# A four-layer graph network on one core: layer 2's running maxima take their scalar from the logits' buffer, 25 pairs ahead

## The chip, the core and the metric

The kernel runs on one core of a Trainium2 chip. Its engines are TensorE (PE in the profile; PEld is its weight load), VectorE (DVE), ScalarE (ACT), GpSimd (POOL) and SyncE (SP, which here only issues DMAs). Each engine works through its own instructions strictly in the order in which they were laid down, and waits on semaphores of the others. The metric is the device time of one execution in microseconds (us); lower is better.

## What is computed

Four layers update x (4096 rows of 256 features) with one adjacency matrix (4096 x 4096): a gated attention layer, a mean over neighbours, a graph attention layer (layer 2) and a dot-product attention layer. The change touches only layer 2:

```
h  = relu(layernorm(x)) @ W
e  = leaky_relu(e_src[:, None] + e_dst[None, :], 0.01)
att = softmax(where(adj > 0, e, -1e12), axis=1)
x  = x + elu(att @ h)
```

Each logit is thus made of one number of its row (src) and one of its column (dst), and the softmax needs, for each row, the maximum over that row's neighbours. Since the leaky slope is monotone, this is decided by the largest dst among the neighbours.

## The kernel before

The kernel is written in a tile framework: the program is traced in Python, and then a scheduler lays each engine's instructions out. Program order is its priority, but an instruction whose inputs or whose buffer are not ready by the scheduler's own reckoning lets later ones go first, so the order in which an engine works can differ from the order in the source. Where an instruction waits on the chip, everything behind it on its engine waits too.

Layer 2 uses the class `Attention` (line 193). The 4096 rows are cut into 8 blocks of 4 row tiles (`RB`), and the columns into 32 tiles of 128 (`NT`), taken two at a time: a *pair* is one block and two column tiles, 16 pairs to a block (`PPB`), 128 pairs in all. A pair goes through these steps:

- `logits` (L348): DVE makes y, two instructions of 128x512 (L355), out of the row of the block (`ab`), the column's scalar (`cdst`) and a row `b` kept in PSUM, which is copied there once a block (L353); GpSimd subtracts the adjacency mask (L359).
- `run` (L361): three pairs later ACT takes the exponential (L387, twice), and PE multiplies by v into four accumulators (L408; 16 matmul records a pair). At a block's edges two pairs are multiplied together. After its last pair come the reciprocals (L417) and `finish2` (L961; L967 on DVE and L971 on ACT empty the accumulators, L975 to L978 do the elu and add to x). There are 5 accumulator buffers for 4 rows of a block.
- y has 8 buffers (`n_y`). A buffer comes free when PE has multiplied it.

The maxima run ahead in `reach` (L273): for each column tile one DVE instruction of 128x512, `run = min(code - dst, run)` (L290 for a block's first column, L292 after), where `dst` is a per-partition scalar, read from the tile that `dst_of` (L225) names. The last one of a block writes `run_sb` in SBUF. Then `top` (L305) is stepped once per pair by `link`: PE transposes `run_sb` (L312), DVE reduces it to one number a row and makes `ab` from it (L316 to L321), PE transposes `ab` (L324), ACT copies it (L327), and two DMAs on ACT's queue write it to memory (L341) and read it back as a row for all partitions (L343). Only then can `logits` of that block begin.

The masks and the codes for the maxima are one tile, `turned`: `stored(b, q)` (L952) loads one of 1 MB, four pairs of one block, by SP's queue into one of 8 buffers. `reach` reads it first, the mask (L359) last, and then the buffer takes the next load.

In `run`, pair n's iteration calls `reach(n + PPB + lead)`, then `logits` of pair n. `lead` is `LEAD` = 7, so the source asks for 16 + 7 = 23 pairs ahead. Ahead of `run`, beside the projections of layer 2, a loop does `reach` for pairs 16 to 22; block 0's were done in layer 1. Nothing but the codes and the run itself holds a `reach` back.

Of the kernel before, what the change touches and what calls it, by code (L numbers as in the profile page):

```python
# [16 lines left out]
ALU = mybir.AluOpType  # L17
AX = mybir.AxisListType
# [23 lines left out]
def kernel(ctx: ExitStack, tc: tile.TileContext, w: dict, out: bass.AP):  # L42
    nc = tc.nc
# [14 lines left out]
    PPB = NT // 2  # L58
# [103 lines left out]
    class Tally:  # L162

        def __init__(self, pool, bufs, lo, hi):
            self.pool, self.bufs = pool, bufs
            self.asked, self.came = [(t, q) for t in range(lo, hi) for q in range(NQ)], []
# [26 lines left out]
    class Attention:  # L193
        def __init__(self, es, tag, slope, lag, n_y, blocks, turned, finish, ps_top=None):
            self.tag, self.slope, self.lag, self.n_y = tag, slope, lag, n_y
            self.turned, self.finish = turned, finish

            self.links = []
            self.blocks = [{"at": at, "n": n} for at, n in blocks]
            vp = es.enter_context(tc.tile_pool(name=f"{tag}_sd", bufs=1))  # L200
            self.sdst = vp.tile([P, NT], F32, name="sdst")
            self.cdst = vp.tile([P, NT], F32, name="cdst")
            self.own_dst, self.held = None, False
            self.ab_d = [
                dram.tile([2, n, P], F32, name=f"{tag}_ab_d{k}") for k, (_, n) in enumerate(blocks)
            ]
            self.picks, self.spread = None, 0
            self.small = es.enter_context(tc.tile_pool(name=f"{tag}_small", bufs=4))
            self.row_p = es.enter_context(tc.tile_pool(name=f"{tag}_rows", bufs=2))
            self.ps_run = es.enter_context(tc.tile_pool(name=f"{tag}_run", bufs=1, space=PSUM))  # L210
            self.ps_top = ps_top or es.enter_context(
                tc.tile_pool(name=f"{tag}_top", bufs=1, space=PSUM)
            )
# [56 lines left out]
            nc.vector.tensor_scalar(self.sdst[:, at], dst, self.slope, None, ALU.mult)  # L270
            nc.vector.tensor_scalar(self.cdst[:, at], dst, 1.0 - self.slope, None, ALU.mult)

        def reach(self, n):  # L273

            b, c = n // PPB, n % PPB * 2
            st = self.blocks[b]
            at, n = st["at"], st["n"]
            if c == 0:  # L280
                st["run"] = self.ps_run.tile([P, RB, P], F32, tag="run", name="run")[:, 0:n, :]
            for j in range(c, c + 2):
                code = self.turned(b, j // QT)[:, :, j % QT, :]
                dst = self.dst_of(slice(j, j + 1))
                to = st["run"]
                if j == NT - 1:
                    to = self.row_p.tile([P, RB, P], F32, tag="run", name="run_sb", bufs=1)
                    to = to[:, 0:n, :]
                if j == 0:
                    nc.vector.tensor_scalar(to, code, dst, None, ALU.subtract)  # L290
                else:
                    nc.vector.scalar_tensor_tensor(  # L292
                        to, code, dst, st["run"], ALU.subtract, ALU.min
                    )
                st["run"] = to
            if c == NT - 2 and not self.held:
                self.links.append(self.top(b))
                if b == 0:
                    self.top_now()
# [61 lines left out]
        def run(self, es, lead, n_acc, ahead=lambda n: None):  # L361

            self.y_p = es.enter_context(tc.tile_pool(name=f"{self.tag}_y", bufs=self.n_y))
            self.ps_b = es.enter_context(
                tc.tile_pool(name=f"{self.tag}_b", bufs=1, space=PSUM)
            )
            ps_acc = es.enter_context(
                tc.tile_pool(name=f"{self.tag}_acc", bufs=n_acc, space=PSUM)
            )
            pairs = [(b, c) for b in range(len(self.blocks)) for c in range(0, NT, 2)]  # L370
            LAG = self.lag
            accs, held = {}, []
            ys = {}
            for n in range(len(pairs) + LAG):
                if n < len(pairs):
                    b, c = pairs[n]
                    ahead(n)
                    if n + PPB + lead < len(pairs):
                        self.reach(n + PPB + lead)
                    y = self.y_p.tile([P, RB, 2, P], F32, tag="y", name="y")  # L380
                    ys[n] = y = y[:, 0 : self.blocks[b]["n"], :, :]
                    self.logits(y, b, c, self.turned(b, c // QT))
                if n >= LAG:
                    b, c = pairs[n - LAG]
                    y = ys.pop(n - LAG)
                    for k in range(2):
                        nc.scalar.activation(  # L387
                            y[:, :, k, :], y[:, :, k, :], AF.Exp,
                            bias=self.sdst[:, c + k : c + k + 1],
                        )  # L390
                    if c == 0:
                        accs[b] = [
                            ps_acc.tile([P, D + 1], F32, tag="acc", name="acc")
                            for _ in range(self.blocks[b]["n"])
                        ]


                    held.append((c, y))
                    edge = NT - 2 - c < 4 or b > 0 and c < 4
                    if edge and len(held) < 2:  # L400
                        self.link()
                        continue
                    terms = [(r, c1 + k, y1) for r in range(len(accs[b]))
                             for c1, y1 in held for k in range(2)]
                    if not edge:
                        terms.sort(key=lambda term: term[1])
                    for r, j, y1 in terms:
                        nc.tensor.matmul(  # L408
                            out=accs[b][r], lhsT=y1[:, r, j % 2, :], rhs=self.v[:, j, 0 : D + 1],
                            start=(j == 0), stop=(j == NT - 1),  # L410
                        )
                    held.clear()
                    if c == NT - 2:
                        done = accs.pop(b)
                        rden = self.small.tile([P, RB], F32, tag="rden", name="rden")
                        for r, acc in enumerate(done):
                            nc.vector.reciprocal(rden[:, r : r + 1], acc[:, 0:1])  # L417
                        self.finish(self.blocks[b]["at"], done, rden)
                self.link()
# [43 lines left out]
    LEAD = 7  # L463
    FIRST = 8
    FRESH = 10
    with ExitStack() as l0:
# [10 lines left out]
        with ExitStack() as es:  # L477
# [24 lines left out]
            n = 2 * RB  # L502
# [458 lines left out]
    def finish2(at, accs, rden):  # L961
# [15 lines left out]
        nc.vector.scalar_tensor_tensor(e, e, 1.0, rows, ALU.min, ALU.add)  # L977
        nc.vector.scalar_tensor_tensor(rows, h, -1.0, e, ALU.max, ALU.add)  # L978

    cuts2 = [(t, RB) for t in range(0, NT, RB)]  # L980
    att2 = Attention(l2, "l2", 0.01, 3, 8, cuts2, None, finish2)
    one2 = l2.enter_context(tc.tile_pool(name="l2_one", bufs=1))
# [9 lines left out]
    def turn2(b, pst):  # L992
        h = one2.tile([P, BT, D], F32, tag="h", name="h")
        for i in range(BT):
            normed2(h[:, i, :], b * BT + i)
        return transposed_block(two2, pst, h, "hT")
# [4 lines left out]
    with ExitStack() as es:  # L1001
# [120 lines left out]
        lead = [gather(t, NB) for t in range(2)]  # L1122
# [14 lines left out]
    with ExitStack() as es:  # L1137
        att2.hold(es)
        turned_p = es.enter_context(tc.tile_pool(name="l2_turned", bufs=8))
        work2 = es.enter_context(tc.tile_pool(name="l2_work", bufs=1))  # L1140
        att2.turned, att2.held = stored, False
        with ExitStack() as ps_:
            pst = ps_.enter_context(tc.tile_pool(name="l2_pst", bufs=3, space=PSUM))
            psm = ps_.enter_context(tc.tile_pool(name="l2_psm", bufs=3, space=PSUM))

            def block2(b):
                hT = hT2.pop(b) if b in hT2 else turn2(b, pst)
                yield
                att2.project(b, hT, psm)
                yield  # L1150

            blocks = [block2(b) for b in range(NB)]
            for _ in blocks.pop(0):
                pass
            att2.links.append(att2.top(0))
            att2.top_now()
            run_staggered(blocks, 1)
            for n in range(PPB, PPB + LEAD):
                att2.reach(n)

        att2.run(es, LEAD, 5)

    l2.close()

# [232 lines left out]
```

## Time and profile before

| | us |
|---|---|
| median of 3 runs (2967.89 to 2974.53) | 2973.59 |
| the profiled execution | 2971.09 |
| its span in the trace (mean granted clock of PE 0.989) | 2969.1 |
| first and last matmul of layer 2's `run` (L408) | 1506.2 to 1995.7 |
| first and last `reach` instruction of layer 2 | 1260.9 to 1880.1 |
| PE, DVE, ACT and POOL busy, whole span | 2862.3, 1904.9, 1260.4, 960.9 |

In the lines below, a row of the timeline gives start, duration, engine, source line, operation, what it writes and reads, its shape, how many were merged, and in brackets how long the engine was idle before it and what released it. A row of the waits gives the total, the count and the longest. DVE's durations overlap by some hundredths at their ends, so the distance between starts is what an instruction costs the engine. PE's busy time is modelled and hides small gaps; the number of matmuls over a stretch of time is a better measure.

### The profile page before, as it was taken

The page shows a single profiled execution, that of the slowest core. Times are in us where ns is not written, and L with a number is a line of the kernel's source. Part 1 is how long each engine was busy: PE and PEld are TensorE (multiplying, and loading weights), DVE is VectorE, ACT ScalarE, POOL GpSimd, SP SyncE. Part 2 cuts the span into 40 slices and gives each one's busy share as a digit, 9 for nine tenths or more (in the row PEclk, how much of TensorE's full clock was granted, in tenths as well). Part 3 has the DMA queues.
Part 4 walks back from the last instruction along what each step waited for, and adds up shares of the span by engine and source line. Part 5 has one row for each costly group of instructions (what it writes and reads, how often), then busy time and mean ns, then how long its engine had stood idle before and what let it go on. Part 6 is the DMA issues. An engine that isn't in the chain of part 4 may idle for free.

```text
span 2969.1 us, 35221 instructions
## 1 busy us (share of the span) xinstructions
PE 2862.3 (96%) x13381; PEld 2336.3 (79%) x13381; DVE 1904.9 (64%) x3491; ACT 1260.4 (42%) x1922; POOL 960.9 (32%) x725
## 2 busy tenths in 40 slices
PE   7999999999999999899999998999999999999999
PEld 6888888856556666788788777888888888888888
DVE  6877767345555554577688888656765666566553
ACT  6765555389963333994354333343111112111111
POOL 6576665545543333321055555540000000000000
PEclk9999999999999999999999999999999999999999
DMA  6966654154520001796432212002111111111100
GB/s 168 224 140 136 137 127 127 44 86 78 78 47 8 8 8 22 192 243 193 144 120 79 78 65 78 29 20 82 36 62 36 38 39 58 39 34 62 34 8 8
DMA packets 109177, 238.62 MB, mean 80 GB/s; under 512 B 10752, under 2 KB 31216, under 8 KB 100304
## 3 DMA queue, kind: packets, MB, share of 16 engines
q1 hardware_dynamic: 68512, 159.34, 15.4%
q0 software_dynamic: 37696, 69.11, 15.0%
q10 hardware_dynamic: 2800, 7.92, 0.8%
q8 instruction: 105, 1.72, 0.2%
q14 instruction: 64, 0.52, 0.1%
HBM read 265.63 MB, written 37.81 MB: 102 GB/s over the span
## 4 chain that ended last, share of the span: by engine, by line
PE 67%; DVE 8%; ACT 7%; POOL 6%; issue 6%; DMA 5%; POOLq 0%; SPq 0%; DVEq 0%; ACTq 0%
PE acc L408 16%; PE acc L1329 15%; PE s L155 15%; PE mm L155 10%; PE acc L1060 8%; POOL y L359 4%; ACT sign L181 3%; DVE run L292 3%; DVE y L355 2%; DMA turned<-codesT 2%; DMA ab_row<-l_ab_d 1%; PE q_ps L155 1%; PE tp L737 1%; DMA a<-in_adj_dram 1%; DMA l_ab_d<-abT_sb 1%
## 5 line engine op out<-in xcount | busy, mean ns | idle before, releaser
L408 PE MATMUL acc<-v,y 128*128 128x257 f32 x4096 | 929.7, 386 | 13.0 <-ACT hp L971 6.3
L408 PEld LDWEIGHTS acc<-v,y 128*128 128x128 f32 x4096 | 777.9, 192 | 126.9 <-ACT hp L971 8.0
L359 POOL TENSOR_TENSOR y<-y,turned 128x1024 f32<-128x1024 f32 (+1 forms) x272 | 549.0, 2039 | 324.8 <-DVE y L355 228.8
L387 ACT ACTIVATE y<-y,sdst 128x512 f32<-128x512 f32 (+1 forms) x544 | 350.3, 689 | 421.2 <-POOL y L359 421.1
L1329 PE MATMUL acc<-v,y 128*128 128x257 f32 x2048 | 454.5, 380 | 0.4 <-DVE rden L1337 0.4
L155 PE MATMUL s<-qT,hT 128*128 128x256 f32 x2048 | 445.2, 379 | 0.7 <-ACT qT L1277 0.7
L1322 ACT ACTIVATE y<-y 128x1024 f32<-128x1024 f32 x128 | 132.2, 1055 | 714.3 <-DVE y L1321 710.0
L155 PEld LDWEIGHTS s<-qT,hT 128*128 128x128 f32 x2048 | 389.0, 190 | 54.2 <-ACT qT L1277 1.4
L1329 PEld LDWEIGHTS acc<-v,y 128*128 128x128 f32 x2048 | 387.1, 190 | 55.9 <-issue 0.8
L355 DVE SCALAR_TENSOR_TENSOR y<-ab_row,cdst,b 128x512 f32<-128x512 f32 (+1 forms) x544 | 366.3, 709 | 64.1 <-PE acc L408 55.9
L181 ACT ACTIVATE sign<-a,limits 128x1024 bf16<-128x1024 bf16 x256 | 293.9, 1148 | 20.7 <-DMA a<-in_adj_dram 15.2
L1291 DVE SCALAR_TENSOR_TENSOR y<-code,s 128x512 f32<-128x512 bf16 x256 | 175.8, 688 | 101.0 <-PE s L155 100.7
L292 DVE SCALAR_TENSOR_TENSOR run<-turned,v,run 128x512 f32<-128x512 bf16 (+1 forms) x270 | 186.5, 691 | 59.9 <-ACT turned L536 56.4
L292 DVE SCALAR_TENSOR_TENSOR run<-turned,dst,run 128x512 f32<-128x512 bf16 x240 | 180.4, 752 | 33.7 <-DMA turned<-codesT 30.1
L1321 DVE TENSOR_TENSOR y<-y,top 128x1024 f32<-128x1024 f32 x128 | 146.2, 1213 | 43.0 <-PE top L1315 43.0
L1298 DVE TENSOR_TENSOR mx<-mx,y 128x512 f32<-128x512 f32 x224 | 154.8, 691 | 7.4
L536 ACT ACTIVATE turned<-cT,log_wide 128x1024 bf16<-128x1024 bf16 x128 | 139.1, 1104 | 41.0 <-PE cT L531 32.1
L174 POOL DMA_DIRECT2D a<-in_adj_dram x128 | 76.5, 599 | 216.1 <-ACT sign L181 161.4
L155 PE MATMUL mm<-kept 128*128 128x512 f32 x288 | 136.8, 615 | 3.3 <-ACT sz L848 2.2
L1060 PE MATMUL acc<-early,eq 128*128 128x512 f32 x512 | 129.0, 401 | 6.9 <-DVE early L457 5.3
L1060 PE MATMUL acc<-late,eq 128*128 128x512 f32 x512 | 122.8, 391 | 0.0
L1060 PEld LDWEIGHTS acc<-early,eq 128*128 128x128 f32 x512 | 96.3, 190 | 30.3 <-DVE early L457 5.5
(236 smaller groups left out, 3013.1 us busy)
## 6 DMA issues: line engine op xcount, KB each, us to landing
turned<-codesT SPq DMA_DIRECT2D x36, 1024.0 KB, 4.8
adj_t<-in_adj_dram POOLq DMA_DIRECT2D x128, 256.0 KB, 5.5
codesT<-turned SPq DMA_DIRECT2D x32, 1024.0 KB, 5.5
a<-in_adj_dram POOLq DMA_DIRECT2D x128, 256.0 KB, 4.8
code<-codesT SPq DMA_DIRECT2D x128, 256.0 KB, 5.8
code<-codesT SPq DMA_DIRECT2D x64, 512.0 KB, 7.2
ab_row<-l_ab_d ACTq DMA_DIRECT2D x14, 512.0 KB, 4.7
xt<-in_x_dram SPq DMA_DIRECT2D x8, 512.0 KB, 3.8
```

Of the source, the lines that this page charges most:

```text
L155: nc.tensor.matmul(out=ps, lhsT=lhsT_of(k), rhs=rhs_of(k), start=(k == 0), stop=(k == n - 1))
L181: nc.scalar.activation(sign, self.came[g], AF.Sign, bias=limits[:, v : v + 1], accum_out=over[:, t, v, q : q + 1],)
L292: nc.vector.scalar_tensor_tensor(to, code, dst, st["run"], ALU.subtract, ALU.min)
L355: nc.vector.scalar_tensor_tensor(y[:, :, k, :], st["ab"][:, 0, :, :], self.cdst[:, c + k : c + k + 1], st["b"], ALU.add, ALU.max,)
L359: nc.gpsimd.tensor_tensor(y, y, mask[:, :, c % QT : c % QT + 2, :], ALU.subtract)
L387: nc.scalar.activation(y[:, :, k, :], y[:, :, k, :], AF.Exp, bias=self.sdst[:, c + k : c + k + 1],)
L408: nc.tensor.matmul(out=accs[b][r], lhsT=y1[:, r, j % 2, :], rhs=self.v[:, j, 0 : D + 1], start=(j == 0), stop=(j == NT - 1),)
L1060: nc.tensor.matmul(out=acc, lhsT=eqs[c // (NT // 2)][:, ts(c % (NT // 2), P)], rhs=v1[c // BT][:, c % BT, :, :], start=(c == 0), stop=(c = ...
L1291: nc.vector.scalar_tensor_tensor(y[:, :, c : c + 2, :], st["code"][:, :, c : c + 2, :], -BIG / UNIT, ps, ALU.mult, ALU.add,)
L1298: nc.vector.tensor_tensor(mx, mx, y[:, :, c : c + 2, :], ALU.max)
L1321: nc.vector.tensor_tensor(part, part, top, ALU.subtract)
L1329: nc.tensor.matmul(out=accs[r], lhsT=st["y"][:, r, c, :], rhs=v3[:, c, :], start=(c == 0), stop=(c == NT - 1),)
```

## The change

In layer 2 alone, `reach` of pair n + 25 no longer reads `dst` from its own tile. When pair n's y buffer is taken, DVE first writes the two scalars that this `reach` needs into the buffer's first two elements, by a `tensor_reduce` with a maximum over one element; the two `reach` instructions read them there, and then `logits` overwrites them. The lead of layer 2 is 9 instead of 7, in the loop ahead of `run` too (pairs 16 to 24).

```diff
-        def reach(self, n):
+        def reach(self, n, tie=None):
...
-                dst = self.dst_of(slice(j, j + 1))
+                dst = self.dst_of(slice(j, j + 1)) if tie is None else tie[:, j - c : j - c + 1]
...
                     ahead(n)
-                    if n + PPB + lead < len(pairs):
-                        self.reach(n + PPB + lead)
                     y = self.y_p.tile([P, RB, 2, P], F32, tag="y", name="y")
+                    m = n + PPB + lead
+                    if m < len(pairs) and self.tied:
+
+                        tie = y[:, 0, 0, 0:2]
+                        at = m % PPB * 2
+                        col = self.dst_of(slice(at, at + 2))
+                        nc.vector.tensor_reduce(
+                            tie, col.rearrange("p (c o) -> p c o", o=1), AX.X, ALU.max
+                        )
+                        self.reach(m, tie)
+                    elif m < len(pairs):
+                        self.reach(m)
                     ys[n] = y = y[:, 0 : self.blocks[b]["n"], :, :]
...
+    LEAD2 = 9
...
-        att2.turned, att2.held = stored, False
+        att2.turned, att2.held, att2.tied = stored, False, True
...
-            for n in range(PPB, PPB + LEAD):
+            for n in range(PPB, PPB + LEAD2):
                 att2.reach(n)
 
-        att2.run(es, LEAD, 5)
+        att2.run(es, LEAD2, 5)
```

More of the change, by code (lines that the diff above doesn't have):

```diff
@@ L203, in __init__ @@
             self.own_dst, self.held = None, False
+            self.tied = False
             self.ab_d = [
```

## The prediction, made before the result was known

> **What bounds the kernel now.** I read the page first: PE carries the span.
>
> ```profile
> PE 2862.3 (96%) x13381; PEld 2336.3 (79%) x13381; DVE 1904.9 (64%) x3491; ACT 1260.4 (42%) x1922; POOL 960.9 (32%) x725
> ```
>
> The change is in layer 2 only, so its stage decides. There the densest stretch of PE has 224 matmul records (L408) in 48.72 us, 0.217 us each; 16 records a pair make 3.47 us a pair, 55.5 us a block of 16 pairs, and 56.1 with the five transposes of `top`. All eight blocks would be 2048 x 0.217 + 7 x 0.55 = 448 us; the stage took 1995.7 - 1506.2 = 489.5. So about 41.5 us can be won at most. To see where they lie I cut the stage at PE's transpose of `ab` (L324), once a block, and asked for busy times (columns: window, its length, then busy PE, PEld, DVE, ACT, POOL).
>
> ```profile
> 1539.80:1597.80 58.00, 56.21 (x264) 48.95 (x263) 53.95 (x82) 24.61 (x38) 35.99 (x17) 1.00 0.23 82
> 1597.80:1662.90 65.10, 56.59 (x261) 48.65 (x261) 55.69 (x84) 23.55 (x37) 34.75 (x16) 0.98 0.20 73
> 1662.90:1728.00 65.10, 58.76 (x261) 50.22 (x261) 52.15 (x79) 23.63 (x37) 34.79 (x16) 0.97 0.20 73
> 1728.00:1793.50 65.50, 59.84 (x261) 51.09 (x262) 52.22 (x79) 23.71 (x37) 34.77 (x16) 0.95 0.21 73
> 1793.50:1858.10 64.60, 58.32 (x261) 49.91 (x261) 52.16 (x79) 23.64 (x37) 34.77 (x16) 0.97 0.21 74
> 1858.10:1915.90 57.80, 57.76 (x262) 50.22 (x263) 38.06 (x59) 23.78 (x37) 34.94 (x17) 0.97 0.08 28
> ```
>
> Two blocks take 58, four take 65. In the four, DVE works 52 to 56 us and idles the rest. DVE's timeline and its waits (1490 to 2030 us) say on what:
>
> ```profile
> 1664.00 2.33 DVE L292 SCALAR_TENSOR_TENSOR run<-turned,dst,run 128x512 f32<-128x512 bf16 x3
> 1671.34 2.34 DVE L292 SCALAR_TENSOR_TENSOR run<-turned,dst,run 128x512 f32<-128x512 bf16 x3 [5.01 <-DMA turned<-codesT]
> 1674.82 0.69 DVE L353 COPY b<-ab_row 128x512 f32<-128x512 f32 x1 [1.15 <-DMA ab_row<-l_ab_d]
> ...
> 1691.09 0.75 DVE L290 TENSOR_SCALAR run<-turned,dst 128x512 f32<-128x512 bf16 x1 [4.12 <-DMA turned<-codesT]
> ...
> 1720.54 2.34 DVE L292 SCALAR_TENSOR_TENSOR run<-turned,dst,run 128x512 f32<-128x512 bf16 x3 [1.63 <-DMA turned<-codesT]
> ```
>
> ```profile
> DVE run L292 <- DMA turned<-codesT: 30.1, 12, 5.0
> ...
> DVE run L290 <- DMA turned<-codesT: 16.1, 4, 4.1
> ```
>
> The maxima have run so far ahead that their codes have no buffer yet: 8 buffers of 4 pairs are 32 pairs, and DVE stands at the head of its queue until GpSimd has used the oldest tile and 4.7 us of load have passed. In the third window that is 7.2 us at L292, 4.1 at L290 and 1.1 for the row: 52.15 + 12.4 = 64.6 of 65.1. PE pays at two places a block:
>
> ```profile
> 1692.56 2.00 PE L408 MATMUL acc<-v,y 128*128 128x257 f32 x8 [1.32 <-ACT hp L971]
> ...
> 1728.04 0.27 PE L324 MATMUL abT<-ident,ab 128*8 128x128 f32 x1 [4.87 <-DVE ab L321]
> ```
>
> The reciprocal behind the wait at 1691.09 frees the accumulators late, and `ab` comes late after the wait at 1720.54.
>
> **The change part by part.** *The order.* The scalar of `reach` n + 25 now exists only once PE has freed pair n's y buffer, so DVE cannot go further than 25 pairs ahead of its own logits. Its tile T is needed first at n = 4T - 25, and its buffer comes free with the mask of pair 4T - 29, four pairs earlier. From the end of the logits of that pair to the arrival of the codes the trace shows 7.15 us (logits end 1713.39, mask to 1715.69, load, `reach` at 1720.54). DVE has three pairs to do in between. Two `reach` and two logits now take 2.77 us (starts 1556.79 to 1559.56), with the new instruction 2.96, so three are 8.9: a slack of 1.7 us. I count the 46.2 us of DMA waits as gone.
>
> *The added instruction.* 103 of them (128 - 25), 16 a block. The nearest row is a reduction to the same 128x2, and its start-to-start cost is that of L320 to L321, independent and small: 0.08 us. The `reach` behind it needs its result; dependent small ones (L318 at 1473.33, L320 at 1473.52) stand 0.19 apart. So 0.19 a pair, 3.0 us a block. The lower end is 0.08 (1.3 us a block); an added instruction on an engine in order cannot cost less than nothing. The upper end is that GpSimd holds it up, as it does a copy of four elements here and L318 at its worst (1.67):
>
> ```profile
> L1029 DVE TENSOR_REDUCE sums<-over x15: 125/160/293, 1201.3 to 1367.1; 128x2 f32<-128x8 f32 x14, 128x36 f32<-128x144 f32 x1
> L801 DVE COPY gain<-bc x8: 170/458/1491, 605.1 to 1085.8; 128x4 f32<-128x4 f32 x8
> ```
>
> A copy would be held: GpSimd is busy 34.8 of 65.1 us, half of its 2.13 us left on average, 0.57 us a time, 9 us a block, and DVE would be back at 64. The Trainium skill speaks on both sides. "VectorE: DVE Perf Modes", Rules for kernel authors, calls tensor_reduce the slowest DVE operation and advises against it on a hot path; "SBUF — State Buffer", Who interferes with whom, says that on this chip it never contends with GpSimd, while copies can. By the first one would take the copy and the 9 us; by the second 3.0. The row of L1029 has no GpSimd arithmetic beside it, so it does not settle this; but L292, which also reads one SBUF tensor, is not held: two of them take 1.54 us from 1710.53 while L359 runs from 1710.79 to 1712.92. I take 3.0 and keep 12 (3 + 9) as upper end.
>
> *The new wait.* The reduction waits for PE; `logits` of that pair waited for the same release before. Behind it on DVE stand two `reach`, the logits, and at edges the reciprocals, on which ACT and then PE depend. A buffer of eight pairs is 8 x 3.47 = 28 us, and from logits to PE there are about 7 (1.4 DVE, 2.1 GpSimd, 1.3 ACT, hand-overs), so some 17 to 20 us of cover: cost nothing, and 1.5 us of `reach` a pair once (the first pair) if the cover is gone.
>
> *The lead of 9.* `run_sb` of a block is asked for two pairs earlier, so `top`, its two transposes, ACT's copy and the two DMAs on ACT's queue start 2 x 3.47 = 6.9 us earlier. They take 17 us from L316 to L353 (1723.45 to 1740.31). The cover is PE's queue of filled buffers. SP's loads are still issued when GpSimd frees a buffer, so SP's queue does not move; POOL's has no DMA here.
>
> *Ahead of `run`.* Before, the scheduler put 27 `reach` there between 1476 and 1501 us, six to every copy L109 that PE waits for (5.2 us a block beside PE's 4.8); after, 18 plus what it still pulls up. Between -2.5 (PE's idle 0.5 x 5) and +1.6 us; I take nothing.
>
> **Sum.** DVE's work in a block is 52.2 + 3.0 = 55.2 us, PE's 56.1: nearly equal, so some loss stays. The first and last windows show what a block costs when DVE waits little: 58.0 and 57.8. I give all blocks 58: 7.1 + 7.1 + 7.5 + 6.6 = 28.3 us off. The profiled execution took 2971.1, so 2942.8; the median lies 2.5 above it: 2945, or 1.0% less. Its own range: all of the 41.5 us (2932) to waits of 2 to 3 us left a block (2956).
>
> **Rivals.**
> - *The slack is too thin.* If codes still come about 1 us late four times a block, a block takes 61.5 to 62: four blocks win 3.5 each, two lose 3.5: -7, so 2966. For it: 1.7 us is little, and the row's arrival bunches DVE's work. Against: it is slack, and a wait once taken widens it.
> - *The change does not do what it says.* The scheduler still lays the order by its own reckoning, and the waits keep their size: 2973, within 6. For it: y buffers come free in its reckoning, not the chip's. Against: the data dependence binds any order.
> - *Slower: no filler while DVE waits for the row.* Before, some ten `reach` stand between the last logits of a block and L353 (1664.0 to 1674.8, 10.8 us). Tied, only as many can go there as y buffers come free, one pair (1.7 us of work) each 3.47 us of PE, so half of a 10 us wait is lost and more if the order places none. If all 10 are lost a block is 55.2 + 10 = 65.2 everywhere: no gain in four blocks, 7 lost in two and in the first: +20, 2994. It decides against the change from (489.5 - 1.56 x 56.5) / 6.44 = 62.3 us a block, that is 7 us of idle DVE a block. Against it: the lead of 9 gives back 6.9 us, and DVE without waits falls behind less.
>
> **How the numbers follow.** A measurement of this kernel can tell about 0.2%, 6 us, from no change. The forecast has 0.60, thin slack 0.15 (two thirds of it beyond 0.2%), no effect 0.10, slower 0.15. So faster 0.70, same 0.15, slower 0.15. Leaving out the slower case and the forecast's far end, the range is 2930 to 2975.
>
> **What would show it.** Right: no DMA wait over 2 us at L290 and L292 in layer 2, 58 us between the L324s, PE's waits for `ab` and `hp` under 2 us, the new reduction at 0.16 us. Wrong: a reduction of 1 us beside L359 (the port), DVE idle before L353 by over 5 us (the row), DVE busy over 58 us a block, or waits for `turned` that stay.

## The result, and the profile after

The median is 2931.8 us (2925.3 to 2938.3, 4 runs) against 2973.1 before: a ratio of 0.986, 95% interval 0.984 to 0.989. The forecast was 2945, range 2930 to 2975. The profiled execution took 2925.3 us, the fastest of the four, its span 2923.4. In the changed kernel all lines of `Attention` and layer 2 have moved: L293 is the old L292, L354 the copy of `b` (L353), L356 the logits (L355), L360 the mask (L359), L419 the matmul (L408), L325 the transpose of `ab` (L324), and L386 is the new reduction.

The page again first, PE and DVE:

```profile
PE 2848.5 (97%) x13381; PEld 2328.8 (80%) x13381; DVE 1915.7 (66%) x3594; ACT 1260.5 (43%) x1922; POOL 959.6 (33%) x725
```

PE's timeline in layer 2 (start, duration, instruction, and in brackets idle time before it):

```profile
1502.02 17.61 PE L419 MATMUL acc<-v,y 128*128 128x257 f32 x80 [2.50 <-ACT y L398]
...
1582.88 0.27 PE L325 MATMUL abT<-ident,ab 128*8 128x128 f32 x1
1582.99 48.72 PE L419 MATMUL acc<-v,y 128*128 128x257 f32 x224
...
1638.92 0.27 PE L325 MATMUL abT<-ident,ab 128*8 128x128 f32 x1
1639.03 48.72 PE L419 MATMUL acc<-v,y 128*128 128x257 f32 x224
...
1695.06 0.27 PE L325 MATMUL abT<-ident,ab 128*8 128x128 f32 x1
```

Every L325 stands 56.0 to 56.2 us after the last one, and none has a bracket: after the stage's first matmul PE does not wait again in it. The stage lasts 1502.0 to 1950.2, 448.2 us, which is the 448 that its matmuls need. It was 489.5, so 41.3 of the 45.8 us between the two profiled executions lie here; of the rest 4.2 are ahead of it, where the starts of the stage scatter between 1501.6 and 1506.2 over the kernels below (e4, e5 and e12, which add work there, apart). The whole stage before and after (window, its length, busy PE, PEld, DVE, ACT, POOL, and PE's mean granted clock as a share of full speed):

```profile
1506.24:1995.74 489.50, 460.88 (x2083) 397.97 (x2084) 370.76 (x593) 190.78 (x293) 278.34 (x134) 0.98 0.17 61
1502.02:1950.20 448.18, 448.18 (x2083) 391.51 (x2084) 381.60 (x688) 190.80 (x293) 276.51 (x134) 1.00 0.19 67
```

Two of the windows between transposes, then DVE's waits (the first row is of before, the others are of the changed kernel), and the reduction:

```profile
1648.00:1704.00 56.00, 56.00 (x262) 48.84 (x261) 53.89 (x94) 23.57 (x36) 33.13 (x17) 1.00 0.22 79
1704.00:1760.00 56.00, 56.00 (x262) 48.80 (x262) 53.65 (x95) 23.57 (x36) 33.96 (x17) 1.00 0.24 85
```

```profile
DVE b L353 <- DMA ab_row<-l_ab_d: 18.3, 7, 8.9
...
DVE b L354 <- DMA ab_row<-l_ab_d: 2.4, 2, 2.2
...
DVE run L293 <- DMA turned<-codesT: 0.4, 1, 0.4
```

```profile
L386 DVE TENSOR_REDUCE y<-dst x103: 135/149/158, 1455.0 to 1838.1; 128x2 f32<-128x2 f32 x103
```

DVE is busy 54 us of 56, its 46.2 us of waits for codes have become 0.4, its 18.3 us for rows 2.4, and none of the 103 reductions took over 0.158 us.

### The profile page after: what moved, and what is told of

Same layout as the page of the kernel before. It is cut to its first block, busy times and chain, and to the rows that moved or that the text cites. A ratio compares the mean times of both kernels' runs of the same rounds, so it can differ in the third digit from the quotient of the medians.

```text
span 2923.4 us, 35308 instructions
## 1 busy us (share of the span) xinstructions
PE 2848.5 (97%) x13381; PEld 2328.8 (80%) x13381; DVE 1915.7 (66%) x3594; ACT 1260.5 (43%) x1922; POOL 959.6 (33%) x725
## 4 chain that ended last, share of the span: by engine, by line
PE 75%; ACT 7%; DVE 5%; issue 5%; POOL 5%; DMA 3%; POOLq 0%; SPq 0%; ACTq 0%; DVEq 0%
PE acc L419 23%; PE acc L1341 15%; PE s L155 15%; PE mm L155 10%; PE acc L1072 8%; ACT sign L181 3%; POOL y L360 2%; DVE run L293 1%; PE cT L542 1%; PE tp L748 1%; DMA ab_row<-l_ab_d 1%; PE q_ps L155 1%; DVE y L356 1%; DMA a<-in_adj_dram 1%; ACT t L764 1%
## 5 line engine op out<-in xcount | busy, mean ns | idle before, releaser
L419 PE MATMUL acc<-v,y 128*128 128x257 f32 x4096 | 918.0, 383 | 5.0 <-ACT y L398 4.3
L419 PEld LDWEIGHTS acc<-v,y 128*128 128x128 f32 x4096 | 771.3, 191 | 113.9 <-ACT y L398 6.3
L360 POOL TENSOR_TENSOR y<-y,turned 128x1024 f32<-128x1024 f32 (+1 forms) x272 | 547.2, 2022 | 282.7 <-DVE y L356 169.4
L356 DVE SCALAR_TENSOR_TENSOR y<-ab_row,cdst,b 128x512 f32<-128x512 f32 (+1 forms) x544 | 368.1, 711 | 70.9 <-PE acc L419 66.1
L293 DVE SCALAR_TENSOR_TENSOR run<-turned,v,run 128x512 f32<-128x512 bf16 (+1 forms) x270 | 186.5, 691 | 57.9 <-ACT turned L547 54.3
L293 DVE SCALAR_TENSOR_TENSOR run<-turned,y,run 128x512 f32<-128x512 bf16 x193 | 145.2, 753 | 3.5 <-DMA turned<-codesT 0.4
```

The lines of the kernel that those rows point to most:

```text
L293: nc.vector.scalar_tensor_tensor(to, code, dst, st["run"], ALU.subtract, ALU.min)
L356: nc.vector.scalar_tensor_tensor(y[:, :, k, :], st["ab"][:, 0, :, :], self.cdst[:, c + k : c + k + 1], st["b"], ALU.add, ALU.max,)
L360: nc.gpsimd.tensor_tensor(y, y, mask[:, :, c % QT : c % QT + 2, :], ALU.subtract)
L419: nc.tensor.matmul(out=accs[b][r], lhsT=y1[:, r, j % 2, :], rhs=self.v[:, j, 0 : D + 1], start=(j == 0), stop=(j == NT - 1),)
```

## The experiments

My theory after the result was the prediction's: the tie keeps the maxima from running into the end of the code buffers, and that is the gain. The rival was that the lead of 9, which starts a block's row two pairs earlier, is what helps. Twelve kernels; "stage" is from the first L419 to the first transpose of layer 3, "codes" and "row" are DVE's waits for `turned` and `ab_row` within it, all from the profiled execution of each.

| kernel | lead, tie | stage us | codes us | row us | median us |
|---|---|---|---|---|---|
| before | 7, none | 489.5 | 46.2 | 18.3 | 2973 |
| changed | 9, y buffer | 448.2 | 0.4 | 2.4 | 2932 |
| e1 | 9, none | 462.5 | 18.1 | 6.6 | 2943 |
| e2 | 7, y buffer | 469.1 | 0 | 35.2 | 2950 |
| e3 | 9, own tiles | 459.4 | 16.8 | 6.7 | 2943 |
| e4 | 9, y buffer, by a copy | 504.5 | 0 | 3.0 | 2986 |
| e5 | 9, none, row made later | 472.6 | 7.7 | 41.2 | 2961 |
| e6 | 11, none | 480.3 | 47.3 | 0 | 2960 |
| e7 | 11, y buffer | 532.0 | 33.0 | 0 | 3013 |
| e8 | 9, y buffer, four reductions | 449.6 | 0 | 2.4 | 2928 |
| e9 | 10, y buffer | 466.6 | 27.6 | 0.2 | 2945 |
| e10 | 11, y buffer, 9 code buffers | 450.0 | 0 | 0 | 2929 |
| e11 | 7, none, 9 code buffers | 477.0 | 15.9 | 29.5 | 2957 |
| e12 | changed, layer 0 tied too | 449.9 | 0.2 | 3.7 | 2966 |

**The two parts apart: e1, the lead alone.**

```diff
-        att2.turned, att2.held, att2.tied = stored, False, True
+        att2.turned, att2.held, att2.tied = stored, False, False
```

> One part alone: the lead of layer 2 is 9, the maxima read dst from its own tile as before. My theory (the gain is that the maxima cannot run past 25 pairs, so DVE never stands before codes that have no buffer): the scheduler still runs them up to the 32 pairs that the buffers hold, DVE's waits for turned stay near 46 us in layer 2, and the time is that of before, 2965 to 2978. Rival (the earlier top, with its two DMAs, is what helps): 2950 or less, with DVE's waits for turned still there.

Measured 2943 (0.990, 0.987 to 0.992). My theory fell as the whole account: the lead alone gives 31 of the 41 us. Not only the row's waits fell (18.3 to 6.6) but also those for codes (46.2 to 18.1):

```profile
DVE run L291 <- DMA turned<-codesT: 10.1, 4, 4.6
DVE run L293 <- DMA turned<-codesT: 8.0, 9, 2.0
DVE b L354 <- DMA ab_row<-l_ab_d: 6.6, 6, 2.3
```

**e2, the tie alone.**

```diff
-    LEAD2 = 9
+    LEAD2 = 7
```

> The other part alone: the maxima take their scalar from the logits' buffer, the lead stays 7, so 23 pairs ahead. My theory: most of the gain, 2932 to 2945; what may come back is DVE waiting for the row of a block, since top starts two pairs (6.9 us) later: up to 2 us a block. Rival (the lead does it): 2960 or more.

Measured 2950 (0.992, 0.990 to 0.994), between the two. Its waits:

```profile
DVE b L354 <- DMA ab_row<-l_ab_d: 35.2, 6, 8.8
PE abT L325 <- DVE ab L322: 10.7, 4, 3.4
```

No wait for codes is left, so that half of the theory holds; but the waits for the row have doubled. This is the mechanism of my slower rival: tied maxima cannot fill the time while DVE waits for the row. Without the lead 18 of the 41 us are missing.

**e3, the reduction without the binding.**

```diff
-                        tie = y[:, 0, 0, 0:2]
+                        tie = self.small.tile([P, 2], F32, tag="tie", name="tie", bufs=8)
```

> The same 103 reductions and the lead of 9, but they write to small tiles of their own (8 buffers), which only the two maxima behind them hold, so nothing ties them to PE. My theory: the scheduler again runs them far ahead and DVE's waits for turned come back: 2965 to 2985, a little above before for the 12 us of reductions. Rival (it is the copy itself, its place in DVE's order or the shape of the read, not the binding to a y buffer): 2945 or less.

Measured 2943 (0.989, 0.988 to 0.991), e1 to the microsecond: 16.8 us of waits for codes against 18.1. The number is the rival's (2945 or less), but it is that of the lead alone: the reduction, its place in the source and reading the scalar elsewhere add nothing to e1. That the place is a y buffer, held by PE, gives the last 11 us.

**e4, a copy in place of the reduction.**

```diff
-                        nc.vector.tensor_reduce(
-                            tie, col.rearrange("p (c o) -> p c o", o=1), AX.X, ALU.max
-                        )
+                        nc.vector.tensor_copy(tie, col)
```

> The changed kernel with a plain copy (tensor_copy, 128x2) in place of the maximum over one element. If a copy is held by GpSimd's arithmetic as my upper end has it (0.57 us a time on average, 9 us a block of DVE), DVE's work goes from 54 to 63 us a block, PE's 56.1 no longer cover it, and layer 2 gets 6.4 blocks x 7 = 45 us longer: about 2975, with copies of up to 2 us. If a copy of two elements is not held: as the changed kernel, 2926 to 2938, all copies under 0.2 us.

Measured 2986 (1.004, 1.003 to 1.006), slower than before and 11 us over the number expected. The timeline, DVE and GpSimd together:

```profile
1659.31 2.13 POOL L360 TENSOR_TENSOR y<-y,turned 128x1024 f32<-128x1024 f32 x1 [3.36 <-DVE y L356]
1659.71 1.75 DVE L386 COPY y<-dst 128x2 f32<-128x2 f32 x1
...
1663.82 2.13 POOL L360 TENSOR_TENSOR y<-y,turned 128x1024 f32<-128x1024 f32 x1 [2.38 <-DVE y L356]
1664.13 1.83 DVE L386 COPY y<-dst 128x2 f32<-128x2 f32 x1
```

Two elements a partition take 1.75 us, until GpSimd's instruction ends (1659.31 + 2.13 = 1661.44; 1659.71 + 1.75 = 1661.46). Of 95 copies in the stage 47 took over 0.3 us, and each of the 47 ends within 0.03 us of the end of a GpSimd instruction. The copies took 76.7 us in all against 14.2 for the reductions: 62.5 us over 5.9 blocks, 10.5 us a block where the prediction had 9. Of the 95 reductions of the changed kernel 52 lie wholly inside an L360 of GpSimd, and none was held. This settles the rule weighed there, as "SBUF — State Buffer" of the Trainium skill has it (Who interferes with whom): a copy can contend with GpSimd, a reduction does not.

**How the lead works: e5, the row made late again.** In the kernel of e1:

```diff
+            if self.tag == "l2":
+                back = self.small.tile([2 * n, P], F32, tag="abT", name="abT_back")
+                nc.scalar.dma_start(out=back, in_=self.ab_d[b].rearrange("v r i -> (v r) i"))
+                nc.scalar.dma_start(out=self.ab_d[b].rearrange("v r i -> (v r) i"), in_=back)
             yield
```

> The lead of 9 without the tie (2943), with the row of a block made later: before it is read for all partitions, abT is read back once and written once more, two more DMAs of some 3.5 us each on ACT's queue, 7 us, about what the lead gained. New theory (there were two causes that feed each other: the row of a block comes late, and while DVE waits for it by the scheduler's reckoning, the maxima are put there and run into the end of the buffers; the lead works through the row alone): back to the state before, 2962 to 2980, DVE's waits for turned over 35 us in layer 2. Rival (the lead works in another way, for one by the two pairs of maxima that are done ahead of the run): stays within 2938 to 2950.

Measured 2961 (0.996, 0.995 to 0.997), a little under the expected band. The rival falls: with the same lead and the same work ahead of `run`, the later row costs 18 us. But the way I had given it falls too: the waits for codes did not come back (7.7 us); DVE stands before the row itself:

```profile
DVE b L358 <- DMA ab_row<-l_ab_d: 41.2, 7, 7.5
```

So the time of the row matters. The two added DMAs do not cost by keeping ACT busy: within the stage PE waits for ACT 1.0 us in all. Splitting DVE's waits by place shows what "before" had: 21.8 of its 46.2 us for codes stood between the last logits of a block and L353 (four of them 5.0 us long, as at 1671.34), while the row was still on its way. With the 18.3 for the row itself DVE stood there 40.1 us, as long as the 41.2 here; only the name of the wait differs.

**e6, a lead of 11 without the tie** (`LEAD2 = 11` in the kernel of e1).

> A lead of 11 without the tie. New theory: the row comes another 6.9 us earlier, so still less of a gap is there to be filled; DVE's waits for turned fall from 18 us to under 10, or they come back from the other side, since the maxima are now asked for 27 pairs ahead and their codes have one pair of time instead of three: 2932 to 2955. My first theory (the tie is what keeps the maxima back): no better than 2943.

Measured 2960 (0.996, 0.995 to 0.998), beyond the new theory's band. "No better than 2943" holds, but says little; what the new theory named as the other side came in full: the row is never waited for, and the codes are, as much as before:

```profile
DVE run L293 <- DMA turned<-codesT: 33.5, 15, 4.6
...
DVE run L291 <- DMA turned<-codesT: 13.8, 4, 4.4
```

So the lead moves DVE's waiting from one end to the other: at 7 rows and codes, at 9 some of both, at 11 codes only.

**The slack: e7 and e9, the tie with a lead of 11 and of 10.**

> The changed kernel with a lead of 11, 27 pairs ahead. By the count of the prediction a tile's buffer comes free at pair 4T - 29 and is wanted at 4T - 27, with one pair (2.9 us) in between for the 7.15 us from the logits' end to the codes: 4.2 us of waiting four times a block, so 54 + 17 = 71 us a block against 56 of PE: about 3000 to 3030, DVE's waits for turned near 100 us. Rival (DVE is far behind or ahead often enough for the slack not to matter): 2930 to 2945.

> The changed kernel with a lead of 10: codes wanted at pair 4T - 26, two pairs (2 x 2.9 = 5.8 us) after the buffer comes free, for a way of 7.15 us, so 1.35 us short four times a block if DVE works back to back. 54 + 5.4 = 59.4 us of DVE a block against 56.1 of PE: 3.3 us x 6.3 = 21 us longer, 2945 to 2955. If the slack is not what decides (DVE waits for PE's buffers in between anyway): 2926 to 2938.

Measured 3013 (1.014, 1.012 to 1.015) and 2945 (0.992, 0.990 to 0.994), both times as the count of pairs had them (the second at the edge). In e7 the waits are not where I put them: 33 us for codes in place of 100, while PE waits 54.7 us for exponentials and DVE 36.5 us for PE at the reduction:

```profile
PE acc L419 <- ACT y L398: 54.7, 27, 3.8
...
DVE y L386 <- PE acc L419: 36.5, 37, 3.3
```

How these waits follow from one another stays open.

**e10, the same lead of 11 with a ninth code buffer** (and 7 y buffers for room).

```diff
-        turned_p = es.enter_context(tc.tile_pool(name="l2_turned", bufs=8))
+        turned_p = es.enter_context(tc.tile_pool(name="l2_turned", bufs=9))
...
-    att2 = Attention(l2, "l2", 0.01, 3, 8, cuts2, None, finish2)
+    att2 = Attention(l2, "l2", 0.01, 3, 7, cuts2, None, finish2)
```

> The tie with the lead of 11 (3013) with 9 buffers for the codes in place of 8, and 7 y buffers in place of 8 to make room. A ninth buffer moves the release of a tile from pair 4T - 29 to 4T - 33, so five pairs lie between release and use in place of one. If it is the missing buffer for the codes that costs at a lead of 11, the time is that of the changed kernel again, 2926 to 2945 (a y buffer less may cost a little). If it is something else that goes with the lead: stays above 2980.

Measured 2929 (0.985, 0.984 to 0.987), 84 us below e7 with one code buffer more and one y buffer less, and neither codes nor rows are waited for. It is the missing code buffer that costs at a lead of 11. With one y buffer less PE is still not held up: the stage is 450.0 us.

**e11, the kernel before with those buffers** (lead 7, no tie).

> The kernel before (lead 7, no tie) with 9 buffers for the codes and 7 for y. The row of a block comes as late as before. If DVE's idle time at codes and rows together is what counts (before 64 us, 2972; so far some 0.65 us of time for each us of it), codes should come in time (46 us gone or nearly) and the row's waits grow towards the 35 us of the tie alone: 2945 to 2960. If the scheduler uses the ninth buffer to run further ahead into its end again: 2965 to 2980.

Measured 2957 (0.995, 0.993 to 0.997). The number is as expected; codes fell to 15.9 and not to nothing, rows rose to 29.5, and the time goes with the sum, 45 us.

**The room on DVE: e8, four reductions for one.**

```diff
+                        for _ in range(4):
                             nc.vector.tensor_reduce(
```

> The changed kernel with the reduction made four times over, into the same two elements: 48 more small DVE instructions a block. At 0.08 to 0.12 us each DVE's work goes from 54 to 58 or 60 us a block, and PE's 56.1 cover it no longer: 2 to 4 us a block, 6.4 blocks, so 2944 to 2957. If DVE has more room than its busy time shows: as the changed kernel, under 2938.

Measured 2928 (0.985, 0.984 to 0.987): no cost at all. The same window as above:

```profile
1648.00:1704.00 56.00, 56.00 (x262) 48.98 (x262) 55.50 (x144) 23.57 (x36) 33.68 (x17) 1.00 0.24 85
```

DVE is busy 55.5 of 56.0 us, and PE all 56. The 48 more instructions a block added 1.6 us of busy time, 0.03 each, and most of that is time in which DVE stood before. The rows of a pair, first in the changed kernel, then here:

```profile
1655.66 0.15 DVE L386 TENSOR_REDUCE y<-dst 128x2 f32<-128x2 f32 x1
1655.85 1.54 DVE L293 SCALAR_TENSOR_TENSOR run<-turned,y,run 128x512 f32<-128x512 bf16 x2
1657.43 1.41 DVE L356 SCALAR_TENSOR_TENSOR y<-ab_row,cdst,b 128x512 f32<-128x512 f32 x2
...
1647.21 0.21 DVE L387 TENSOR_REDUCE y<-dst 128x2 f32<-128x2 f32 x2
1647.40 0.75 DVE L293 SCALAR_TENSOR_TENSOR run<-turned,y,run 128x512 f32<-128x512 bf16 x1
1648.06 0.15 DVE L387 TENSOR_REDUCE y<-dst 128x2 f32<-128x2 f32 x1
1648.19 0.76 DVE L293 SCALAR_TENSOR_TENSOR run<-turned,y,run 128x512 f32<-128x512 bf16 x1
...
1650.30 0.21 DVE L387 TENSOR_REDUCE y<-dst 128x2 f32<-128x2 f32 x2
```

Two maxima of one pair start 0.79 us apart with a reduction between them (1647.40 to 1648.19) as without (two such steps from 1655.85 to 1657.43), and the pair takes 3.09 us (1647.21 to 1650.30) with four reductions as with one (1655.66 to 1658.75).

**A better version? e12, layer 0 tied too.**

```diff
+            att.tied = True
             att.run(es, LEAD, 4, ahead)
```

> The changed kernel with the same tie in layer 0 too, where the lead stays 7 and the codes come from PE and ACT and not from memory (DVE waits there 54 us for them). If maxima placed too early hold up DVE in layer 0 as well: 2880 to 2925. If the codes of layer 0 are simply late for any order, or DVE is not what bounds it, the reductions and the waits for y buffers only add: 2930 to 2960.

Measured 2966 (0.998, 0.997 to 0.999): 34 us worse than the changed kernel, and slower than either expectation. Layer 2 is unhurt (449.9); it starts 36 us later, 1538.1. Most of this is lost at the start of layer 0: PE's fourth L325 stands at 210.7 us, in the changed kernel at 187.1. DVE's waits for the codes from ACT in layer 0 did not fall (58.7 at L293, 54.3 before the tie), and waits for PE at the reduction came on top; which of these costs the time was not tested:

```profile
DVE run L293 <- ACT turned L547: 58.7, 15, 4.9
DVE y L386 <- PE acc L419: 25.1, 27, 9.7
```

No kernel here beats the changed one beyond the scatter of its runs (2925 to 2938); e8 and e10 equal it.

## Why the prediction was right, and where it was not

**The bound and the end.** Right: 41.5 us were to be won at most, and 41.3 were.

**The mis-sized term** is "I give all blocks 58". Six windows measured 56.0 to 56.2, so 376.1 became 336.6 us, 39.6 off, not 28.3; the other 1.7 lie outside these windows. I had taken 58.0 and 57.8 from the two cheap blocks as a floor, but each held a loss of its own: in the first PE waits 1.79 us at L324; in the last PE is busy all the time, but its granted clock is half from 1858.2 for 3.4 us, 1.7 us lost (the row has 0.97). I had also kept a loss because DVE (55.2) and PE (56.1) were nearly equal. DVE was busy 54, and e8 shows that even 55.5 costs nothing with eight y buffers between the two engines.

**What PE lost before.** I read PE's cost at full clock and passed over the clock in the rows above. Of the 41.3 us, 28.6 are PE's waits; the other 12.7 are the same 2083 matmuls taking longer (460.9 against 448.2 us busy), because the granted clock was half in six stretches, 23.8 us together: after the wait of 4.87 us, 10 matmuls fall into the 3.4 us from 1728.5, and 17 into the 3.4 us from 1732.0. In every kernel here each such stretch of the stage begins during a wait of PE or at most 1.4 us after its end; all 25 waits of over 3.2 us had one, of the shorter ones some. That the wait brings on the low clock is read from this order and not tested. The 448 us, PE's waits and half of the time at half clock add up to the stage within 1 us in twelve of the fourteen kernels, within 6 in e4 and e7.

**The order.** The waits for codes are gone with the tie, as forecast (0.4 us; 0 in e2), and e7, e9 and e10 confirm the count of pairs: three pairs of slack at 9, one buffer decides at 11. But that the tie does away with all 46.2 us was luck in part: only 24.4 of them were for the tie to win, and the 21.8 between a block's logits and its row are the late row's (e5). The tie alone turns these into waits for the row. That stretch was also misread for the slower rival: from 1664.0 to 1674.8 six maxima stand in it, not ten, and DVE waits 6.2 us.

**The lead of 9** is the step I got wrong. I costed it at nothing, and named "PE's queue of filled buffers" as the cover for the row. e2 shows what that cover was worth: with the tie and without the lead DVE waits 35.2 us for rows, and 18 us of the time come back. e1 gives 31 us to the lead alone, e2 23 to the tie alone; together they give 41, not 54, since both take from the same idle time of DVE. The slower rival's mechanism was thus real; what kept it from deciding is the 6.9 us of the lead, which I had only counted against it in a clause.

**The account that fits.** DVE stood for two reasons. Before a late row (its waits for codes there counted in): 40.1 us before, 6.6 with the lead alone, 35.2 with the tie alone, 2.4 with both. For codes elsewhere: 24.4, 18.1, 0 and 0.4. So the lead wins most of the first and the tie the second, and that is why the lead alone also cuts the waits for codes. Over the kernels without a held copy and with layer 0 as it was (e4 and e12 apart), time goes with the sum: 64.5 us and 2973, 49 and 2961, 47 and 2960, 45 and 2957, 35 and 2950, 28 and 2945, 24 to 25 and 2943, 2.8 and 2932: some two thirds of a microsecond for each. This is a fit and no law: e7, with 33 us and 3013, is far off it. DVE, busy 54 us to PE's 56, has little room to make up for idle time.

**The added reduction.** 0.149 us each where 0.16 was forecast, never held; a pair mostly takes 2.90 or 3.09 us of DVE, by its order, where 2.96 was forecast. A term was missing: the logits overwrite elements that the maxima read, and where they come right behind, they start 0.79 us after the second maximum (52 of 53 times between 1530 and 1860 us), in e3, with the scalars elsewhere, mostly 0.66. **The new wait**: DVE stood 3.1 us in all at L386, PE never within the stage; costing it at nothing was right. **Ahead of `run`**: 27 `reach` instructions were placed there again, 18 of the loop's and 9 tied ones, for which y buffers were free. I took nothing; the stage starts 4.2 us earlier, but the starts of the other kernels scatter as widely, so how much of it the change gives stays open.

## What to carry to other kernels

When an engine at 95% of the bounding one idles in front of loads, add up its idle time by cause: removing one cause can make another larger, and only both together reach the bound. Ask of each wait what would be waited for if it were gone, and look at the granted clock after each wait of PE. How far work runs ahead can be fixed through data, by letting it read something from a buffer that the paced engine frees; set the lead so that both the buffer it needs and the result it produces have time, and count that time in units of the loop. Pick for such a marker an instruction that GpSimd does not hold up.

## What the runs showed of the hardware that I had not expected

- A copy of 128x2 on DVE was held up to 2.0 us by a GpSimd instruction, half of the time; a reduction of the same size, from and to the same places, never (0.158 us at most), though 52 of 95 ran inside a GpSimd instruction.
- Small DVE instructions between two of which the second needs the first's result cost next to nothing: three more reductions a pair left the pair at 3.09 us (e8), though the profile shows each as 0.15 us.
- During or just after the longer waits of PE its granted clock was half, for 3.4 or 6.8 us at a time (23.8 us of the stage before, none after). Some 12 of the 41.3 us won are matmuls that no longer run at half clock.
